# One step of Strassen's algorithm, in its seven-product form, for x times W1 in a gated cross-attention kernel

## Chip, cores, metric

The kernel runs on one core of one Trainium2 chip. The metric is the device time of one execution in microseconds. The kernel before takes 1226.47 us (median of three runs, 1226.44 to 1226.92). All data are fp32.

## The reference, cut to what matters

With x of (8, 1024, 1024), a memory of (8, 64, 512), W_mem (1024, 512) and W_gate (1024, 2048):

```python
memory_proj = einsum('bme,de->bmd', memory, W_mem)
scores = einsum('bnd,bmd->bnm', x, memory_proj) / sqrt(D)
attn = softmax(scores, axis=-1)
memory_context = einsum('bnm,bmd->bnd', attn, memory_proj)
gate_input = concatenate([x, memory_context], axis=-1)
gate = sigmoid(einsum('bnf,df->bnd', gate_input, W_gate) + b_gate)
fused = x + gate * memory_context
out = fused * rsqrt(mean(fused**2, axis=-1) + 1e-6) * norm_w
```

The gate's product splits into x times W1 (the half of W_gate for x) and memory_context times W2. The second is folded: mp times W2 plus the bias is computed once per batch, so that attn multiplies a table of 64 rows.

## The kernel before

**Setup.** TensorE transposes the memory (L133), projects it (L152, tile pm, result mpT), transposes the projection back (L169, into rows 0 to 63 of the table mg) and multiplies it by W2 (L181, tile pg2, from the tiles w2_0 and w2_1; VectorE adds the bias in L190 into rows 64 to 127 of mg). W1 is loaded into one tile, w1_sb.

**The loop.** The rows of x are handled in 32 pairs of 128-row tiles, pair q being 256 rows (t = 0 and 1). For each pair:

- `transpose_x`: VectorE turns x round in 32 by 32 blocks into xt, with 8 instructions (L203). Two buffers hold xt.
- `scores`: 16 matmuls into psT (L214), copied by ScalarE into sT (L222).
- `softmax`: a transpose on TensorE into sc (L228), then on VectorE the maximum mx (L230), the difference e (L232), on ScalarE the exponential (L233), on VectorE the sum den (L235), its reciprocal rden (L237) and attn (L240, two instructions).
- `transpose_attn`: two transposes on TensorE into pa (L249), copied by ScalarE into attnT (L251).
- `fuse`, once per t: for each of two halves h of 512 columns, 8 matmuls of x with W1 into a PSUM bank pg (L266). Then, for each h, two matmuls with a depth of 64 rows: attnT with the projection into pc (L278) and attnT with the folded table into pg (L279). ScalarE takes the sigmoid of pg (L284), VectorE multiplies it by pc (L285), adds x (L286), and ScalarE sums the squares (L287).
- `norm`: ScalarE's square root (L293), VectorE's reciprocal (L294) and scaling (L296), and the two stores.

**Order.** Nothing in the kernel before fixes an engine's order except the order in which the code is written and the scheduler of the tile framework, which may move an instruction up into a gap. In iteration q the code issues `transpose_x` and `scores` of pair q+1, `fuse(q, 0)`, `softmax` of q+1, `fuse(q, 1)`, `transpose_attn` of q+1 and `norm(q)`. Each engine runs its own queue in order.

One fp32 matmul stands in the trace as two matmul records, so a group of 8 matmuls is 16 records, and a pair's 32 matmuls with W1 are 64.

Of the kernel before, what the change touches and what calls it, by code (L numbers as in the profile page):

```python
# [14 lines left out]
P = 128  # L15
# [4 lines left out]
def tile_gated_cross_attention_rmsnorm(  # L20
# [25 lines left out]

    nc = tc.nc
# [7 lines left out]
    KE = E // P  # L55
    H = 512
# [9 lines left out]
    xgpool = ctx.enter_context(tc.tile_pool(name="xgpool", bufs=4))  # L66
    xtpool = ctx.enter_context(tc.tile_pool(name="xtpool", bufs=2))
    work = ctx.enter_context(tc.tile_pool(name="work", bufs=2))
# [35 lines left out]
    bias_sb = const.tile([P, D], F32, name="bias_sb")  # L104
# [9 lines left out]
    w1_sb = const.tile([P, KD, D], F32, name="w1_sb")  # L114
    for k in range(0, KD, 4):
        for i in range(4):
            nc.sync.dma_start(
                w1_sb[32 * i : 32 * (i + 1), k : k + 4, :], w1r[i][:, k : k + 4, :]
            )
    nw_sb = const.tile([P, D], F32, name="nw_sb")  # L120
# [73 lines left out]

    for q in range(2):
        xqs[q] = load_xq(q)
    xts, sTs, attns, attnTs = {}, {}, {}, {}
# [9 lines left out]

    def scores(q):
# [3 lines left out]
        for k in range(KD):  # L212
            for t in range(2):
                nc.tensor.matmul(  # L214
                    ps[t * M : (t + 1) * M, :],
                    mpT[:, k, b * M : (b + 1) * M],
                    xt[:, k, t * P : (t + 1) * P],
                    start=(k == 0),
                    stop=(k == KD - 1),
                )  # L220
# [4 lines left out]
    def softmax(q):  # L225

        sc = ps_sc.tile([P, 2, M], F32, tag="sc", name=f"sc{q}")
        nc.tensor.transpose(sc.rearrange("p t m -> p (t m)"), sTs.pop(q), ident)  # L228
# [16 lines left out]
    def transpose_attn(q):  # L245
        attn = attns.pop(q)
        pa = ps_sc.tile([P, 2, P], F32, tag="sc", name=f"pa{q}")
        for t in range(2):
            nc.tensor.transpose(pa[:, t, :], attn[:, t, :, :].rearrange("p i m -> p (i m)"), ident)  # L249
        attnT = small.tile([P, 2, P], F32, tag="attnT", name=f"attnT{q}")  # L250
        nc.scalar.copy(attnT, pa)  # L251
# [4 lines left out]
    def fuse(q, t):  # L256

        b = q // PPB
        if t == 0:
            sss[q] = small.tile([P, 2], F32, tag="ss", name=f"ss{q}")  # L260
        xg, xt, attnT, ss = xgs[q], xts[q], attnTs[q], sss[q]
        pgs = []
        for h in range(NH):
            pg = ps_gate.tile([P, H], F32, tag="gate", name=f"pg{q}_{t}_{h}")
            for k in range(KD):
                nc.tensor.matmul(  # L266
                    pg,
                    xt[:, k, t * P : (t + 1) * P],
                    w1_sb[:, k, h * H : (h + 1) * H],
                    start=(k == 0),  # L270
                    stop=False,
                )
            pgs.append(pg)
        pcs = []
        for h in range(NH):
            cols = slice(h * H, (h + 1) * H)
            pc = ps_ctx.tile([P, H], F32, tag="ctx", name=f"pc{q}_{t}_{h}")
            nc.tensor.matmul(pc, attnT[0:M, t, :], mg[0:M, b, cols], start=True, stop=True)  # L278
            nc.tensor.matmul(pgs[h], attnT[M:P, t, :], mg[M:P, b, cols], start=False, stop=True)  # L279
            pcs.append(pc)  # L280
        gate = work.tile([P, D], F32, tag="gate", name=f"gate{q}_{t}")
        for h in range(NH):
            cols = slice(h * H, (h + 1) * H)
            nc.scalar.activation(gate[:, cols], pgs[h], AF.Sigmoid)  # L284
            nc.vector.tensor_tensor(gate[:, cols], gate[:, cols], pcs[h], ALU.mult)  # L285
        nc.vector.tensor_tensor(xg[:, t, :], xg[:, t, :], gate, ALU.add)  # L286
        nc.scalar.activation(gate, xg[:, t, :], AF.Square, accum_out=ss[:, t : t + 1])  # L287
# [13 lines left out]

    transpose_x(0)
    scores(0)
    softmax(0)
    transpose_attn(0)
    for q in range(2):
        xgs[q] = load_xg(q)
    for q in range(NQ):
# [4 lines left out]
        if nxt:  # L313
            transpose_x(q + 1)
            scores(q + 1)
        fuse(q, 0)
        if nxt:
            softmax(q + 1)
        fuse(q, 1)
        if nxt:  # L320
# [28 lines left out]
```

## Time and profile before

| | |
|---|---|
| median of three runs | 1226.47 us |
| profiled execution, its own time | 1225.63 us |
| its span, first to last instruction | 1223.9 us |
| mean granted TensorE clock | 0.995 of full speed |
| TensorE matmul busy | 1195.8 us, 98% |
| VectorE busy | 385.8 us, 32% |
| ScalarE busy | 361.1 us, 30% |
| GpSimd busy | 0.7 us |
| HBM traffic | 93 GB/s over the span |

Spans are measured from the first instruction to the last; the execution's own time is 1.73 us longer. In the rows, PE is TensorE's matmul, PEld its weight load, DVE VectorE, ACT ScalarE, POOL GpSimd, SP the queue that issues the DMAs. A row of instructions gives line, engine, operation, output and inputs, partitions and elements, the count, busy time and mean duration, and then the idle time before them with what ended it. Matmuls overlap: the records of one run may be longer than the distance between their starts, and the distance is what a run costs.

### The profile page before, as it was taken

To read this page: it belongs to the slowest core of one execution; us is meant where nothing else is said; L and a number is where in the kernel's file an instruction comes from. 1 tells how busy PE (TensorE), PEld (TensorE's weight loads), DVE (VectorE), ACT (ScalarE), POOL (GpSimd) and SP (SyncE) were. 2 spreads that over 40 slices of the span, in tenths; PEclk is the share of its full clock that TensorE was granted. 3 is DMA by queue.
4 is the path that set the end of the run, shared out by engine and by line. 5 is a ranking of instruction groups with operands and counts; after the bars stand their busy time and mean duration, and the time that the engine had idled before them with its cause. 6 is when DMAs were issued, how large, how long until landed. Compare 5 with 4: busy or idle time off the path is not lost.

```text
span 1223.9 us, 9771 instructions
## 1 busy us (share of the span) xinstructions
PE 1195.8 (98%) x3920; PEld 541.1 (44%) x3920; DVE 385.8 (32%) x764; ACT 361.1 (30%) x531; POOL 0.7 (0%) x7
## 2 busy tenths in 40 slices
PE   7999999999999999999999999999999999999996
PEld 3444444444444444444444444444444444444442
DVE  2113333233323323233333332333233332333322
ACT  0300332333223332333223322333233323332232
POOL 0000000000000000000000000000000000000000
PEclk9999999999999999999999999999999999999998
DMA  9925132233332222333332222333322223330000
GB/s 247 217 86 138 45 84 90 91 104 103 103 103 75 76 83 78 103 103 103 103 103 69 61 94 86 104 103 103 103 83 77 74 83 98 103 103 35 35 35 34
DMA packets 57469, 113.88 MB, mean 93 GB/s; under 512 B 3920, under 2 KB 36688, under 8 KB 57424
## 3 DMA queue, kind: packets, MB, share of 16 engines
q1 hardware_dynamic: 57424, 113.26, 31.3%
q8 instruction: 31, 0.51, 0.2%
q14 instruction: 14, 0.11, 0.0%
HBM read 79.69 MB, written 33.55 MB: 93 GB/s over the span
## 4 chain that ended last, share of the span: by engine, by line
PE 91%; DVE 7%; ACT 1%; DMA 1%; issue 0%; DVEq 0%; SPq 0%; ACTq 0%
PE pg L266 73%; DVE xt L203 7%; PE pc L278 5%; PE psT L214 5%; PE pg L181 4%; PE pm L152 2%; PE sc L228 1%; DMA wm_sb<-in_w_mem_t 1%; ACT mg L172 0%; PE pt_mp L169 0%; DVE xg L296 0%; ACT L293 0%; DVE xg L286 0%; DVEq L345 0%; ACT gate L287 0%
## 5 line engine op out<-in xcount | busy, mean ns | idle before, releaser
L266 PE MATMUL pg<-w_sb,xt 128*128 128x512 f32 x2048 | 894.8, 594 | 0.0
L266 PEld LDWEIGHTS pg<-w_sb,xt 128*128 128x128 f32 x2048 | 385.5, 191 | 463.8 <-issue 463.8
L284 ACT ACTIVATE gate<-pg 128x512 f32<-128x512 f32 x128 | 76.5, 597 | 649.9 <-PE pg L279 649.9
L203 DVE STREAM_TRANSPOSE xt<-xq 128x256 f32<-128x256 f32 x256 | 87.4, 408 | 299.8 <-PE pg L266 299.8
L278 PE MATMUL pc<-mg,attnT 64*128 64x512 f32 x256 | 126.8, 615 | 0.0
L279 PE MATMUL pg<-mg,attnT 64*128 64x512 f32 x256 | 126.8, 615 | 0.0
L230 DVE TENSOR_REDUCE mx<-sc 128x2 f32<-128x128 f32 x32 | 9.4, 293 | 324.0 <-PE sc L228 324.0
L285 DVE TENSOR_TENSOR gate<-gate,pc 128x512 f32<-128x512 f32 x128 | 81.1, 671 | 33.0 <-ACT gate L284 33.0
L214 PE MATMUL psT<-xt,mpT 128*64 128x128 f32 x1024 | 77.1, 278 | 8.2 <-DVE xt L203 8.2
L284 ACT ACT_TABLE_LOAD x63 | 80.8, 1283 | 1.1
L296 DVE SCALAR_TENSOR_TENSOR xg<-xg,rstd,nw_sb 128x1024 f32<-128x1024 f32 x64 | 79.4, 1282 | 1.1
L286 DVE TENSOR_TENSOR xg<-xg,gate 128x1024 f32<-128x1024 f32 x64 | 78.1, 1221 | 1.1
L287 ACT ACTIVATE gate<-xg 128x1024 f32<-128x1024 f32 x64 | 67.7, 1057 | 35.5 <-DVE xg L286 31.2
L278 PEld LDWEIGHTS pc<-mg,attnT 64*128 64x128 f32 x256 | 42.8, 186 | 78.7 <-issue 78.7
L214 PEld LDWEIGHTS psT<-xt,mpT 128*64 128x64 f32 x1024 | 61.5, 137 | 24.4 <-DVE xt L203 12.5
L181 PE MATMUL pg<-w,mpT 128*128 128x512 f32 x128 | 55.6, 592 | 0.0
L222 ACT COPY sT<-psT 128x128 f32<-128x128 f32 x32 | 8.5, 266 | 125.5 <-PE psT L214 125.5
L279 PEld LDWEIGHTS pg<-mg,attnT 64*128 64x128 f32 x256 | 42.8, 186 | 0.0
L293 ACT ACT_TABLE_LOAD x32 | 41.1, 1283 | 0.6
L233 ACT ACT_TABLE_LOAD x31 | 39.8, 1283 | 0.6
L181 PEld LDWEIGHTS pg<-w,mpT 128*128 128x128 f32 x128 | 24.0, 190 | 28.7 <-issue 28.7
L294 DVE RECIPROCAL rstd<-rstd 128x2 f32<-128x2 f32 x32 | 5.3, 166 | 90.4 <-ACT rstd L293 90.4
(32 smaller groups left out, 207.6 us busy)
## 6 DMA issues: line engine op xcount, KB each, us to landing
xq<-in_x SPq DMA_DIRECT2D x128, 256.0 KB, 4.4
xg<-in_x SPq DMA_DIRECT2D x32, 1024.0 KB, 4.8
out<-xg SPq DMA_DIRECT2D x64, 512.0 KB, 2.7
w<-in_w_gate_t SPq DMA_DIRECT2D x8, 512.0 KB, 19.0
w_sb<-in_w_gate_t SPq DMA_DIRECT2D x8, 512.0 KB, 20.1
wm_sb<-in_w_mem_t SPq DMA_DIRECT2D x2, 1024.0 KB, 8.5
mem_sb<-in_mem SPq DMA_DIRECT2D x1, 1024.0 KB, 5.5
bias_sb<-in_b_gate SPq DMA_DIRECT2D x1, 512.0 KB, 10.8
```

Of the source, the lines that this page charges most:

```text
L181: nc.tensor.matmul(pg, mpT[:, k, q * P : (q + 1) * P], w2_sb[h][:, k, :], start=(k == 0), stop=(k == KD - 1),)
L203: nc.vector.transpose(xt[:, :, 32 * s : 32 * (s + 1)], xq[:, s, :].rearrange("p (j r) -> p j r", r=32))
L214: nc.tensor.matmul(ps[t * M : (t + 1) * M, :], mpT[:, k, b * M : (b + 1) * M], xt[:, k, t * P : (t + 1) * P], start=(k == 0), stop=(k == K ...
L266: nc.tensor.matmul(pg, xt[:, k, t * P : (t + 1) * P], w1_sb[:, k, h * H : (h + 1) * H], start=(k == 0), stop=False,)
L278: nc.tensor.matmul(pc, attnT[0:M, t, :], mg[0:M, b, cols], start=True, stop=True)
L279: nc.tensor.matmul(pgs[h], attnT[M:P, t, :], mg[M:P, b, cols], start=False, stop=True)
L284: nc.scalar.activation(gate[:, cols], pgs[h], AF.Sigmoid)
L285: nc.vector.tensor_tensor(gate[:, cols], gate[:, cols], pcs[h], ALU.mult)
L286: nc.vector.tensor_tensor(xg[:, t, :], xg[:, t, :], gate, ALU.add)
L287: nc.scalar.activation(gate, xg[:, t, :], AF.Square, accum_out=ss[:, t : t + 1])
L293: nc.scalar.activation(rstd, ss, AF.Sqrt, bias=eps_sb, scale=1.0 / D)
L296: nc.vector.scalar_tensor_tensor(xg[:, t, :], xg[:, t, :], rstd[:, t : t + 1], nw_sb, ALU.mult, ALU.mult)
```

## The change

A pair's product is a 2 by 2 block product: A11 and A12 are the first tile's rows with the first and the second half of the 1024 features (4 slices of 128 each), A21 and A22 the second tile's; B11 to B22 are the quarters of W1 (4 slices by 512 columns). Before, it takes 8 block products of 4 matmuls each. Now it takes 7, by Winograd's form of Strassen's step:

- of W1, once, in the setup: t1 = B12 - B11, t2 = B22 - t1, t3 = B22 - B12 (over B12's buffer), all three on GpSimd, and t4 = B21 - t2 on VectorE. t1 and t2 share the buffer that w2_0 had, and t4 has that of w2_1;
- of x, per pair, on VectorE (`sums`): s1 = A21 + A22, s2 = s1 - A11, s3 = A11 - A21, s4 = A12 - s2;
- the products go into three PSUM banks k1, k2, k3. k1 holds A11 B11 and then, in addition, A12 B21; k2 holds s2 t2, then also s3 t3, then also A22 t4; k3 holds s1 t1, then also s4 B22;
- the part sums that several results need are taken out of PSUM while a bank stays open: ScalarE copies k1 after its first product into p1; VectorE computes u2 = p1 + k2, u3 = p1 + k2 (after k2's second product), u3 += k3, p1 += k2 and u2 += k3;
- since a bank goes into more than one result, attnT gets a third slot, the difference of the two tiles' attn, so that the folded table's product, added to a bank that two results share, comes out right.

All matmuls and transposes of the loop are kept in program order on TensorE. `transpose_x`, `scores` and `softmax` of the next pair are called from within `fuse`, after the second, the fourth and the sixth product. Buffers change: xgpool 4 to 3, work 2 to 3 with the bias in one of its buffers during the setup, a new spool with one buffer for each of s1 to s4, p1, u2 and u3. W1 comes in 16 loads of 256 KB where it came in 8 of 512 KB. The result's residual add is now issued for t = 1 first and t = 0 after it.

The core of the diff:

```diff
-    for k in range(0, KD, 4):
+    for k, h in ((0, 0), (0, 1), (1, 1), (1, 0)):
+        t = const.tile([P, KH, H], F32, name=f"b{k + 1}{h + 1}")
...
+    nc.gpsimd.tensor_tensor(t1, b12, b11, ALU.subtract)
+    nc.gpsimd.tensor_tensor(t2, b22, t1, ALU.subtract)
+    nc.gpsimd.tensor_tensor(b12, b22, b12, ALU.subtract)
+    t3 = b12
+    t4 = big.tile([P, KH, H], F32, tag="big", name="t4")
+    nc.vector.tensor_tensor(t4, b21, t2, ALU.subtract)
...
+    def sums(q):
+        a11, a12, a21, a22 = blocks(q)
...
+        nc.vector.tensor_tensor(s1, a21, a22, ALU.add)
+        nc.vector.tensor_tensor(s2, s1, a11, ALU.subtract)
+        nc.vector.tensor_tensor(s3, a11, a21, ALU.subtract)
+        nc.vector.tensor_tensor(s4, a12, s2, ALU.subtract)
...
-        attnT = small.tile([P, 2, P], F32, tag="attnT", name=f"attnT{q}")
-        nc.scalar.copy(attnT, pa)
+        attnT = small.tile([P, 3, P], F32, tag="attnT", name=f"attnT{q}")
+        nc.scalar.copy(attnT[:, 0:2, :], pa)
+        nc.vector.tensor_tensor(
+            attnT[M:P, 2, :], attnT[M:P, 0, :], attnT[M:P, 1, :], ALU.subtract
+        )
...
+        def product(bank, lhsT, rhs, start):
+            for k in range(KH):
+                mm(bank, lhsT[:, k, :], rhs[:, k, :], start and k == 0, k == KH - 1)
...
+        product(k1, a11, b11, True)
...
+        nc.scalar.copy(p1, k1)
...
+        product(k2, s2, t2, True)
...
+        nc.vector.tensor_tensor(u2, p1, k2, ALU.add)
+        between[0]()
+        product(k1, a12, b21, False)
+        product(k2, s3, t3, False)
...
+        nc.vector.tensor_tensor(u3, p1, k2, ALU.add)
+        between[1]()
...
+        product(k3, s1, t1, True)
+        pc11 = attend(k1, 0, 0, 0)
+        pc22 = attend(k3, 1, 1, 1)
+        nc.vector.tensor_tensor(u3, u3, k3, ALU.add)
+        gated(k1, pc11, 0, 0)
+        gated(u3, pc22, 1, 1)
+        product(k2, a22, t4, False)
+        between[2]()
+        product(k3, s4, b22, False)
+        pc21 = attend(k2, 1, 0, 1)
+        pc12 = attend(k3, 0, 1, 2)
+        nc.vector.tensor_tensor(p1, p1, k2, ALU.add)
+        gated(p1, pc21, 1, 0)
+        nc.vector.tensor_tensor(u2, u2, k3, ALU.add)
+        gated(u2, pc12, 0, 1)
+        for t in (1, 0):
+            residual(t)
```

Three places show what moves. The first is TensorE over a pair, pair 1 before, from the next pair's scores on (a name's first number is the pair, those of pg and pc then give t and h):

```order
L214 MATMUL psT2_547<-xt2_538,mpT_152 64x128 x16
L266 MATMUL pg1_0_0_567<-w1_sb_103,xt1_414 128x512 x8
L266 MATMUL pg1_0_1_576<-w1_sb_103,xt1_414 128x512 x8
L278 MATMUL pc1_0_0_585<-mg_201,attnT1_522 128x512
L279 MATMUL pg1_0_0_567<-mg_201,attnT1_522 128x512
L278 MATMUL pc1_0_1_588<-mg_201,attnT1_522 128x512
L279 MATMUL pg1_0_1_576<-mg_201,attnT1_522 128x512
L228 MATMUL sc2_598<-ident_114,sT2_564 128x128
L266 MATMUL pg1_1_0_612<-w1_sb_103,xt1_414 128x512 x8
L266 MATMUL pg1_1_1_621<-w1_sb_103,xt1_414 128x512 x8
```

And pair 2 of the changed kernel, from its first product on (t12 holds t1 and t2, b12 holds t3; the second product's s2 is s2_2). All calls of `mm` carry the helper's line, L229:

```order
L229 MATMUL k1_2_720<-b11_106,xt2_597 128x512 x4
L229 MATMUL k2_2_727<-t12_360,s2_2_696 128x512 x4
L229 MATMUL k1_2_720<-b21_121,xt2_597 128x512 x4
L229 MATMUL k2_2_727<-b12_111,s3_2_697 128x512 x4
L229 MATMUL psT3_753<-xt3_734,mpT_166 64x128 x16
L229 MATMUL k3_2_772<-t12_360,s1_2_695 128x512 x4
L229 MATMUL pc2_0_0_777<-mg_215,attnT2_692 128x512
L229 MATMUL k1_2_720<-mg_215,attnT2_692 128x512
L229 MATMUL pc2_1_1_780<-mg_215,attnT2_692 128x512
L229 MATMUL k3_2_772<-mg_215,attnT2_692 128x512
L229 MATMUL k2_2_727<-t4_364,xt2_597 128x512 x4
L282 MATMUL sc3_792<-ident_128,sT3_770 128x128
```

After these come s4 B22 into k3 (4 matmuls), four more attention matmuls and the next pair's pa. The 32 matmuls with W1 have become 28, in groups of 4, and psT has moved from behind pa into the middle of the pair.

The second place is VectorE at the end of a pair, before, from a pair's first maximum to its last transposes:

```order
L230 TENSOR_REDUCE mx2_600<-sc2_598 128x2
L285 TENSOR_TENSOR gate1_0_591<-gate1_0_591,pc1_0_0_585 128x512
L285 TENSOR_TENSOR gate1_0_591<-gate1_0_591,pc1_0_1_588 128x512
L232 TENSOR_TENSOR e2_602<-sc2_598,mx2_600 128x128
L286 TENSOR_TENSOR xg1_405<-xg1_405,gate1_0_591 128x1024
L235 TENSOR_REDUCE den2_605<-e2_602 128x2
L237 RECIPROCAL rden2_607<-den2_605 128x2
L240 TENSOR_TENSOR attn2_609<-e2_602,rden2_607 128x2x64 x2
L203 STREAM_TRANSPOSE xt3_662<-xq3_531 128x8x32 x8
```

And in the changed kernel, in pair 2:

```order
L236 STREAM_TRANSPOSE xt4_871<-xq4_710 128x8x32
L285 TENSOR_REDUCE mx3_794<-sc3_792 128x2
L236 STREAM_TRANSPOSE xt4_871<-xq4_710 128x8x32
L287 TENSOR_TENSOR e3_796<-sc3_792,mx3_794 128x128
L236 STREAM_TRANSPOSE xt4_871<-xq4_710 128x8x32 x6
L290 TENSOR_REDUCE den3_799<-e3_796 128x2
L292 RECIPROCAL rden3_801<-den3_799 128x2
L258 TENSOR_TENSOR s4_3_835<-xt3_734,s2_3_833 128x512
L295 TENSOR_TENSOR attn3_803<-e3_796,rden3_801 128x2x64 x2
L377 TENSOR_TENSOR p1_2_725<-p1_2_725,k2_2_727 128x512
L379 TENSOR_TENSOR u2_2_732<-u2_2_732,k3_2_772 128x512
```

The transposes of xt for the pair after the next (xt4 while pair 2 runs) now stand among the softmax of pair 3, and s4 of pair 3 stands ahead of its attn. The sums s3, s1 and s2 of pair 3 stand earlier in the pair.

The third place is the step from the setup into the loop: on TensorE before,

```order
L181 MATMUL pg2_1_3_335<-w2_1_98,mpT_152 128x512 x8
L214 MATMUL psT0_365<-xt0_356,mpT_152 64x128
L266 MATMUL pg0_0_0_443<-w1_sb_103,xt0_356 128x512
L214 MATMUL psT0_365<-xt0_356,mpT_152 64x128 x15
L266 MATMUL pg0_0_0_443<-w1_sb_103,xt0_356 128x512
L228 MATMUL sc0_384<-ident_114,sT0_382 128x128
L266 MATMUL pg0_0_0_443<-w1_sb_103,xt0_356 128x512 x3
L249 MATMUL pa0_398<-ident_114,attn0_395 128x128 x2
L266 MATMUL pg0_0_0_443<-w1_sb_103,xt0_356 128x512 x3
```

and in the changed kernel:

```order
L198 MATMUL pg2_1_3_349<-w2_1_101,mpT_166 128x512 x8
L229 MATMUL psT0_385<-xt0_376,mpT_166 64x128 x16
L282 MATMUL sc0_404<-ident_128,sT0_402 128x128
L305 MATMUL pa0_418<-ident_128,attn0_415 128x128 x2
L229 MATMUL k1_0_446<-b11_106,xt0_376 128x512 x4
```

The first pair's matmuls with W1, which filled the gaps of its softmax, now stand behind its last transpose. On VectorE the same step is now

```order
L207 TENSOR_TENSOR mg_215<-pg2_1_3_349,bias_sb_94 64x512 x2
L220 TENSOR_TENSOR t4_364<-b21_121,t12_360 128x2048
L236 STREAM_TRANSPOSE xt0_376<-xq0_366 128x8x32 x8
L255 TENSOR_TENSOR s1_0_424<-xt0_376 128x512
L257 TENSOR_TENSOR s3_0_426<-xt0_376 128x512
L256 TENSOR_TENSOR s2_0_425<-s1_0_424,xt0_376 128x512
L258 TENSOR_TENSOR s4_0_427<-xt0_376,s2_0_425 128x512
L285 TENSOR_REDUCE mx0_406<-sc0_404 128x2
```

where before mg's last two rows were followed at once by the transposes of xt0 and these by mx0: t4 and the four sums have come between.

124 lines of the change are left out of this document (78 added, 46 removed).

## Prediction

> **What bounds the kernel now.** I read the page's busy times and the chain that ended last first:
>
> ```profile
> PE 1195.8 (98%) x3920; PEld 541.1 (44%) x3920; DVE 385.8 (32%) x764; ACT 361.1 (30%) x531; POOL 0.7 (0%) x7
> PE 91%; DVE 7%; ACT 1%; DMA 1%; issue 0%; DVEq 0%; SPq 0%; ACTq 0%
> ```
>
> TensorE has no gaps worth speaking of, and the end hangs on it nearly everywhere. So the question is what one pair costs there. Busy times of overlapping matmuls overstate that, so I cut one pair in the middle of the run at the points where TensorE changes from one kind of work to the next, and read the lengths of the stretches (the second column):
>
> ```profile
> 559.64:573.57 13.93, 13.93 (x34) 6.00 (x33) 3.13 (x4) 4.28 (x6) 0.00 (x0) 1.00 0.70 211
> 573.57:575.49 1.92, 1.92 (x10) 0.69 (x10) 0.00 (x0) 0.60 (x1) 0.00 (x0) 1.00 0.03 9
> 575.49:575.65 0.16, 0.16 (x3) 0.16 (x2) 0.00 (x0) 0.05 (x1) 0.00 (x0) 1.00 0.00 0
> 575.65:589.48 13.83, 13.83 (x33) 5.90 (x33) 3.67 (x9) 4.58 (x6) 0.00 (x0) 1.00 0.00 0
> 589.48:591.40 1.92, 1.92 (x10) 0.69 (x9) 1.81 (x6) 0.60 (x1) 0.00 (x0) 1.00 0.00 0
> 591.40:591.77 0.37, 0.37 (x5) 0.20 (x3) 0.37 (x2) 0.26 (x1) 0.00 (x0) 1.00 0.00 0
> 591.77:594.26 2.49, 2.32 (x33) 1.90 (x32) 2.46 (x5) 0.61 (x2) 0.00 (x0) 1.00 0.26 81
> sum 34.62, PE 34.45 PEld 15.54 DVE 11.44 ACT 10.96 POOL 0.00; mean PE 4.92 PEld 2.22 DVE 1.63 ACT 1.57 POOL 0.00
> ```
>
> The same for one pair near the end of the run:
>
> ```profile
> 1113.73:1148.36 34.63, 34.45 (x117) 15.55 (x116) 11.45 (x24) 10.96 (x16) 0.00 (x0) 1.00 0.08 31
> ```
>
> The first seven stretches are, in order: 32 records of x times W1, four attention matmuls, the transpose sc, 32 records again, four attention matmuls, pa, and psT. A pair costs 34.62 us, and 34.63 at the end, so it holds over the loop. VectorE works 11.44 us of it and ScalarE 10.96: both have room. What one record of x times W1 costs is read from the starts of the weight loads, the first and the last of 30 in the first stretch:
>
> ```profile
> 560.17 0.19 PEld L266 LDWEIGHTS pg<-w_sb,xt 128*128 128x128 f32 x1 [0.24 <-issue]
> ...
> 572.62 0.19 PEld L266 LDWEIGHTS pg<-w_sb,xt 128*128 128x128 f32 x1 [0.24 <-issue]
> ```
>
> 12.45 / 29 = 0.429 us. 32 of them are 13.73 us of the 13.93, and the other 0.2 is the change to the matmuls of 64 rows behind them.
>
> **The change, part by part. Four matmuls fewer per pair.** 28 in place of 32, so 8 records fewer: 8 x 0.429 = 3.43 us a pair. The groups of 4 have the same shapes, 128 by 128 by 512, and a change of bank inside the 13.83 us stretch (after 16 records) shows no gap, so I charge nothing for the six changes of bank.
>
> **psT in another place.** Today psT follows pa and waits there for the transposes of x, which are only freed to start when the last matmul with W1 is through:
>
> ```profile
> PEld psT L214 <- DVE xt L203: 12.5, 30, 0.4
> ```
>
> That is 0.40 us a pair. In the changed order the transposes for a pair are done half a pair ahead of its psT, so the wait goes. In return there is one more change of shape on TensorE, from products to psT, which I take at the 0.2 above (bounds 0 and 0.2). A pair then costs 34.62 - 3.43 - 0.40 + 0.2 = 31.0 us if nothing makes TensorE wait.
>
> **Does anything make it wait?** VectorE gets nine instructions of 512 elements and one small one per pair. The groups they resemble:
>
> ```profile
> L285 DVE TENSOR_TENSOR gate<-gate,pc 128x512 f32<-128x512 f32 x128 | 81.1, 671 | 33.0 <-ACT gate L284 33.0
> L286 DVE TENSOR_TENSOR xg<-xg,gate 128x1024 f32<-128x1024 f32 x64 | 78.1, 1221 | 1.1
> L284 ACT ACTIVATE gate<-pg 128x512 f32<-128x512 f32 x128 | 76.5, 597 | 649.9 <-PE pg L279 649.9
> L296 DVE SCALAR_TENSOR_TENSOR xg<-xg,rstd,nw_sb 128x1024 f32<-128x1024 f32 x64 | 79.4, 1282 | 1.1
> L287 ACT ACTIVATE gate<-xg 128x1024 f32<-128x1024 f32 x64 | 67.7, 1057 | 35.5 <-DVE xg L286 31.2
> L160 ACT COPY mpT<-pm 128x512 f32<-128x512 f32 x4 | 2.3, 586 | 32.8 <-PE pm L152 32.8
> ```
>
> 9 x 0.67 + 0.2 = 6.2, so VectorE comes to 17.6 of 31 us, and ScalarE with p1's copy to 11.5. Totals don't decide; the waits between do. I count from T, when pa of a pair starts. TensorE then runs pa to T+0.4, the first two products to T+7.2, needs p1 out of k1 there, and needs u2 out of k2 at T+10.7. VectorE has behind T: u2 += k3 of the pair before (0.7), two gate multiplications (1.3), two residual adds (2.4), attnT's difference (0.2): done at T+4.8. ScalarE's copy of p1 is queued behind the squares of the first residual, which is ready at about T+3.4: 3.4 + 1.1 + 0.6, so T+5.2 against 7.2. u2 then waits for the second product at T+7.2 and is there at T+8, against 10.7. The scaling (two instructions of 1.28 us) ends at T+11; u3 waits for the fourth product at T+14.1 anyway. s1 of the next pair waits for this pair's k3 product to be through, at T+19.8, with s2 behind it, and u3 += k3, queued behind them, starts when k3's attention is in, at T+22, ends at T+22.7, and is needed at T+25.5. All of this has 2 us or more to spare.
>
> The close place is the end of the pair. The last reader of xt is A22 t4; call its end E. From there VectorE has the transposes for the pair after the next, with the softmax among them, then s4, then attn, which pa needs. The rows of today:
>
> ```profile
> 575.85 0.29 DVE L230 TENSOR_REDUCE mx<-sc 128x2 f32<-128x128 f32 x1 [10.22 <-PE sc L228]
> 577.25 0.28 DVE L232 TENSOR_TENSOR e<-sc,mx 128x128 f32<-128x128 f32 x1
> 578.59 0.28 DVE L235 TENSOR_REDUCE den<-e 128x2 f32<-128x128 f32 x1
> 578.90 0.17 DVE L237 RECIPROCAL rden<-den 128x2 f32<-128x2 f32 x1
> 579.10 0.49 DVE L240 TENSOR_TENSOR attn<-e,rden 128x128 f32<-128x128 f32 x2
> 589.59 2.73 DVE L203 STREAM_TRANSPOSE xt<-xq 128x256 f32<-128x256 f32 x8 [9.99 <-PE pg L266]
> ```
>
> 0.11 until VectorE sees E (589.59 against 589.48), 2.73, then 0.29 + 0.28 + 0.28 + 0.17, s4 at 0.67, attn at 0.49, and some 0.2 of steps between: attn is there at E+5.2. TensorE reaches pa after sc (0.26 with its change), the last product (3.43 + 0.2) and four attention matmuls (1.92): E+5.8. So 0.6 us are left, and pa does not wait; p1 += k2, which is queued behind attn, is 0.3 us late, and that falls into the 2 us above. I take 0 and keep up to 0.5 us a pair for the range.
>
> **Loads.** SP's queue issues a pair's stores, then xg, then the next xq but one; each lands a good half pair ahead of its use, since transfers (the column ahead of the last in the stretches above) fill 0.70 of the first 13.93 us and little of the rest. The smaller xgpool makes xg wait for the stores of the pair three back, whose data are needed 30 us later: nothing.
>
> **The setup.** W1's sums need w2_0 free. The chain of waits and three windows (clock granted in the third column from the end) give it:
>
> ```profile
> 47.23 52.38 PE pg L181 x122
> 73.00:100.00 27.00, 26.59 (x62) 11.41 (x61) 5.07 (x8) 0.00 (x0) 0.00 (x0) 1.00 0.00 1
> 100.00:104.00 4.00, 1.40 (x3) 0.79 (x4) 3.73 (x10) 0.00 (x0) 0.00 (x0) 0.80 0.00 0
> 104.00:108.00 4.00, 4.00 (x34) 2.40 (x33) 0.00 (x0) 0.27 (x1) 0.00 (x0) 0.77 0.79 175
> ```
>
> L181 ends at 99.6; its second half, 64 records, takes 27.4 us, so w2_0 is free at 72.2, and no load is under way from 73 on. GpSimd's three subtractions of 2048 elements have no row here. The nearest is this, 0.29 us for 128 elements:
>
> ```profile
> masks.py:199 POOL TENSOR_SCALAR_AFFINE_SELECT ident<-ident 128x128 f32<-128x128 f32 x1 | 0.3, 294 | 0.0
> ```
>
> That makes 16 x 0.29 = 4.7 each as the upper bound; VectorE's 1.22 for 1024 makes 2.4 the lower one. I take 4.7, the engine's own row: 72.2 + 14.1 = 86.3, well ahead of t4 on VectorE at 101, so they cost nothing up to 14 us each for t1 and t2. The Trainium skill, GPSIMD Engine Reference, section Elementwise — side-by-side cycle accounting, gives 4497 ns for such an addition of 2048 fp32 elements, twice VectorE's time; by that the third would end at 85.7, and no run here shows it yet.
>
> What costs is VectorE's queue and TensorE's order, where the setup meets the loop:
>
> ```profile
> 101.03 2.73 DVE L203 STREAM_TRANSPOSE xt<-xq 128x256 f32<-128x256 f32 x8
> 103.19 2.08 PE L266 MATMUL pg<-w_sb,xt 128*128 128x512 f32 x2
> 105.19 2.24 PE L214 MATMUL psT<-xt,mpT 128*64 128x128 f32 x30
> 107.47 0.27 ACT L222 COPY sT<-psT 128x128 f32<-128x128 f32 x1 [57.47 <-PE psT L214]
> 108.33 0.27 PE L228 MATMUL sc<-ident,sT 128*128 128x128 f32 x1
> 110.15 0.49 DVE L240 TENSOR_TENSOR attn<-e,rden 128x128 f32<-128x128 f32 x2
> ```
>
> t4 (2 x 1.22) stands ahead of the transposes: they run from 103.5 to 106.2. psT to 108.5, sT to 108.9; from sc to the end of attn today 110.64 - 108.33 = 2.3, so attn at 111.3 and pa at 111.4. The four sums (2.7) end at 108.9, just covered by psT and sT. Until then TensorE does nothing with W1. It has also idled, and the clock falls: 0.80 and 0.77 in the windows above, 8 us with some 1.7 us lost. I charge 1.7 for the first products. The Trainium skill, TensorE: Matmul & The Clock Gate, section What's actually happening, halves the clock after an idle window of some 3.4 us and gives it back after as long a busy one; by that the loss is 1.7, or 3.4 if the wait for attn cools it again, and the sum below would be as it is or 1.7 more. The two records of 2.08 us at 103.19 agree with half speed.
>
> **The end.** The last TensorE record now starts at 1211.40:
>
> ```profile
> 1211.40 0.59 PE L279 MATMUL pg<-mg,attnT 64*128 64x512 f32 x1
> 1218.95 1.53 SPq L299 DMA_DIRECT2D out<-xg  x2
> ```
>
> From 1211.9 to 1223.9 it is 12.0 us. Now u2 += k3 comes ahead of the last sigmoid (0.7) and the residual of t = 1 ahead of that of t = 0 (1.24): 14.0.
>
> **The sum.** 111.4 + 1.7 + 32 x 31.0 - 2.5 (the last pair has no psT, sc and their change) + 14.0 = 1116.6 us of span. Done the same way, before gives a start of 106.8 for its 34.62 us pairs, so the setup costs 6.3 more, the end 2.0 more, and the pairs 115.8 less. The profiled execution lies 1.73 above its span (1225.63 and 1223.9) and the median 0.84 above that: **1119 us**.
>
> **The rivals.** *The softmax is late* (15%): VectorE's chain from E outlasts TensorE's 5.8 us, because instructions in that chain run longer beside the new PSUM reads or wait longer for each other. Each 10% on the chain is 0.5 us; beyond the 0.6 to spare it costs 31 times the excess. At +30% that is 31 x 1.0 = 31, so 1150; the case spans 1130 to 1175. For it: the chain has ten links, and only runs of eight were seen undisturbed. Against: the same instructions vary little now.
>
> *Short products break the stream* (6%): each group of 4 starts with a gap like the 0.2 us where TensorE changes shape. Six more a pair: 32 x 1.26 = 40, so 1159. Against it, no gap at the bank changes within 32 records.
>
> *Slower* (2%): the same chain from E at more than 1.8 times its length. From 5.2 to over 9.4 us TensorE waits more than 3.6 us a pair, which eats all that the pairs gain. At twice the length: 31 x 4.6 = 143, so 1262. Every instruction of it would have to slow as much, and none has been seen to.
>
> *A setup that holds the loop back* (4%): GpSimd at over 14 us an instruction keeps t4, and the transposes behind it, waiting. At 20 us each, 11 us: 1130. That the change doesn't do what it says is excluded: the order of the instructions holds the 28 matmuls.
>
> **The numbers.** The forecast as worked out has 72%, with its own range of 1110 (no cold clock, no new change of shape) to 1130 (0.4 us a pair of waiting); 1% is left for a still faster pair. For 8 in 10 the range takes in the nearer half of the late softmax: 1109 to 1146. A difference of about 0.2% is what a measurement of this kernel can tell. All cases but the slow one and a small remainder are far below that line: faster 97%, the same 1%, slower 2%.
>
> **What would show it.** Right: 56 records of products in a pair, pairs of 31.0 us, no idle time on TensorE ahead of pa, GpSimd's last subtraction over before 101 us, pa of the first pair at about 111. Wrong: pairs over 32 us; pa waiting for attn would be the late softmax, gaps ahead of each product's first weight load the broken stream, and products waiting for VectorE or for p1 a wait that I have dismissed.

## The result, and the profile after

The changed kernel takes 1106.9 us (median of four runs, 1106.69 to 1108.91) against 1226.45 us (1226.25 to 1226.92) for the kernel before: a ratio of 0.9028, with a 95% interval of 0.9013 to 0.9044. It is faster, as forecast, and by more: 119.6 us where 107 were forecast, 2 us under the low end of the range. Its profiled execution took 1106.89 us, with a span of 1105.1; the forecast for the span was 1116.6.

The page's span, busy times and chain that ended last, of the changed kernel:

```profile
span 1105.1 us, 9666 instructions
PE 1074.8 (97%) x3664; PEld 484.3 (44%) x3664; DVE 586.2 (53%) x1085; ACT 376.3 (34%) x563; POOL 14.2 (1%) x10
PE 96%; DVE 1%; ACT 1%; DMA 1%; issue 0%; DVEq 0%; SPq 0%; ACTq 0%
```

TensorE still sets the end, now for 96% of the chain, and VectorE's share of it has gone from 7% to 1% although VectorE works half as long again. One pair in the middle of the changed kernel, from the start of its pa to the start of the next pa, cut at the first record of each new kind of work on TensorE (the second column is the length, then busy time and count of PE, PEld, DVE, ACT and POOL):

```profile
572.18:572.46 0.28, 0.28 (x5) 0.28 (x4) 0.16 (x1) 0.28 (x1) 0.00 (x0) 1.00 1.16 209
572.46:586.29 13.83, 13.83 (x35) 5.90 (x33) 7.62 (x10) 5.47 (x10) 0.00 (x0) 1.00 0.48 129
586.29:588.18 1.89, 1.89 (x33) 1.72 (x32) 1.29 (x2) 0.00 (x0) 0.00 (x0) 1.00 0.74 173
588.18:591.81 3.63, 3.63 (x10) 1.44 (x8) 0.00 (x0) 1.55 (x2) 0.00 (x0) 1.00 0.49 199
591.81:593.73 1.92, 1.92 (x9) 0.69 (x8) 1.38 (x2) 0.60 (x1) 0.00 (x0) 1.00 0.00 0
593.73:597.26 3.53, 3.53 (x10) 1.58 (x9) 1.97 (x3) 1.91 (x2) 0.00 (x0) 1.00 0.00 0
597.26:597.37 0.11, 0.11 (x2) 0.10 (x1) 0.00 (x0) 0.00 (x0) 0.00 (x0) 1.00 0.00 0
597.37:600.90 3.53, 3.53 (x10) 1.34 (x8) 3.40 (x12) 1.59 (x2) 0.00 (x0) 1.00 0.00 0
600.90:602.82 1.92, 1.92 (x9) 0.69 (x8) 1.81 (x5) 0.02 (x1) 0.00 (x0) 1.00 0.48 148
sum 30.64, PE 30.64 PEld 13.73 DVE 17.63 ACT 11.42 POOL 0.00; mean PE 3.40 PEld 1.53 DVE 1.96 ACT 1.27 POOL 0.00
```

In order: pa, four products (32 records), psT, the fifth product, attention, the sixth product, sc, the seventh, attention. TensorE is busy for all of the 30.64 us; before, 0.17 of 34.62 were idle, all in the stretch of psT. Set beside the stretches of before, the 3.98 us that a pair has lost are these:

| per pair | before | after | change |
|---|---|---|---|
| 8 records of products fewer, at 0.429 | 64 | 56 | -3.43 |
| what the product stretches hold beyond 0.429 a record | 0.30 | 0.50 | +0.20 |
| psT | 2.49 | 1.89 | -0.60 |
| pa | 0.37 | 0.28 | -0.09 |
| sc | 0.16 | 0.11 | -0.05 |

The first line is what was forecast. The third was forecast at 0.40. The second was forecast at 0.20, too, but for psT's new place alone, and the last two lines, which the forecast did not look at, give most of it back.

### The profile page after: what moved, and what is told of

Its sections match the earlier page's. It is cut to its first block, busy times and chain, and to the rows that moved or that the text cites. A ratio compares the mean times of both kernels' runs of the same rounds, so it can differ in the third digit from the quotient of the medians.

```text
span 1105.1 us, 9666 instructions
## 1 busy us (share of the span) xinstructions
PE 1074.8 (97%) x3664; PEld 484.3 (44%) x3664; DVE 586.2 (53%) x1085; ACT 376.3 (34%) x563; POOL 14.2 (1%) x10
## 4 chain that ended last, share of the span: by engine, by line
PE 96%; DVE 1%; ACT 1%; DMA 1%; issue 0%; DVEq 0%; SPq 0%; ACTq 0%
PE k L229 71%; PE pc L229 11%; PE psT L229 6%; PE pg L198 5%; PE pm L169 2%; PE pa L305 1%; DMA wm_sb<-in_w_mem_t 1%; ACT mg L189 0%; PE sc L282 0%; DVE xt L236 0%; DVE xg L346 0%; DVE t L220 0%; PE pt_mp L186 0%; DVE xg L391 0%; ACT L388 0%
## 5 line engine op out<-in xcount | busy, mean ns | idle before, releaser
L229 PE MATMUL k<-t,s 128*128 128x512 f32 x512 | 233.4, 598 | 0.0
L229 PE MATMUL k<-b,xt 128*128 128x512 f32 x512 | 231.9, 596 | 0.0
L229 PE MATMUL k<-b,s 128*128 128x512 f32 x512 | 230.2, 592 | 0.0
L229 PEld LDWEIGHTS k<-b,s 128*128 128x128 f32 x512 | 94.9, 190 | 116.6 <-issue 116.6
L229 PEld LDWEIGHTS k<-t,s 128*128 128x128 f32 x512 | 94.7, 190 | 112.9 <-issue 112.9
L229 PEld LDWEIGHTS k<-b,xt 128*128 128x128 f32 x512 | 95.4, 191 | 108.2 <-issue 108.2
L229 PE MATMUL k<-mg,attnT 64*128 64x512 f32 x256 | 126.8, 615 | 0.0
L229 PE MATMUL pc<-mg,attnT 64*128 64x512 f32 x256 | 126.8, 615 | 0.0
L229 PE MATMUL k<-t,xt 128*128 128x512 f32 x256 | 118.4, 605 | 0.0
L255 DVE TENSOR_TENSOR s<-xt 128x512 f32<-128x512 f32 x32 | 22.2, 692 | 131.5 <-PE k L229 131.4
L229 PEld LDWEIGHTS pc<-mg,attnT 64*128 64x128 f32 x256 | 42.8, 186 | 78.7 <-issue 55.9
L229 PEld LDWEIGHTS k<-t,xt 128*128 128x128 f32 x256 | 46.0, 189 | 70.2 <-issue 46.7
L229 PE MATMUL psT<-xt,mpT 128*64 128x128 f32 x1024 | 65.3, 280 | 5.8 <-DVE xt L236 5.8
L229 PEld LDWEIGHTS psT<-xt,mpT 128*64 128x64 f32 x1024 | 57.1, 139 | 30.5 <-issue 29.5
```

The costliest lines, as they stand in the source:

```text
L229: nc.tensor.matmul(o, lhsT, rhs, start=start, stop=stop, skip_group_check=True)
L255: nc.vector.tensor_tensor(s1, a21, a22, ALU.add)
```

## The experiments

Two theories stood after the result. *The wait*: psT's place was worth 0.6 us a pair, because it waited there for the transposes of x, and the rest is eight records. *The rival*: more of the gain comes from elsewhere, from the shorter stream or from VectorE's new order, and psT's place was worth the 0.40 that its row showed.

### psT moved in the kernel before

Only this is changed: psT of the next pair comes between the two column halves of the first tile's product, so that x is turned round by then.

```diff
-            scores(q + 1)
-        fuse(q, 0)
+        fuse(q, 0, (lambda q=q + 1: scores(q)) if nxt else None)
...
+            if h == 0 and mid is not None:
+                mid()
```

> The kernel before, with 8 products, but with the next pair's psT between the two halves of the first tile instead of right behind pa. Theory (the changed kernel's extra gain lies in psT: clear of the transposes of x its stretch costs 1.9 us where it costs 2.49 before, and pa 0.1 less): pairs of 34.62 - 0.60 - 0.09 + 0.1 for one more change of shape = 34.0 us, time about 1226 - 18 = 1208. Rival (the forecast's term was right, 0.40 for the wait less 0.2 for the change of shape, and the rest of the gain comes from the products): pairs of 34.4, time about 1220.

Measured: 1208.35 us (1206.28 to 1209.17) against 1224.44 on the same chip, ratio 0.9861 (0.9844 to 0.9878). Two psT, a pair apart, in the chain of that kernel (start, length):

```profile
555.40 1.90 PE psT L214 x32
...
589.43 1.90 PE psT L214 x32
```

A pair is 589.43 - 555.40 = 34.03 us, 0.59 less than the 34.62 of before, and in the same chain the two halves around psT are 6.87 and 7.06, together the 13.93 that they were. So the whole difference is psT's 2.49 that became 1.90, and psT between products costs nothing for a change of shape. The rival's 34.4 falls. In the time, 31 x 0.59 would be 18.3 us. The profiled execution, 1206.28 us, lies 18.2 below 1224.44 and the median 16.1, since the four runs spread over 2.9 us; what varies is taken up below.

### psT right behind pa, in the changed kernel

If only the wait counted, the old place must cost nothing once x is ready there.

```diff
-            fuse(q, (first, second, third))
+            first()
+            second()
+            fuse(q, (nothing, nothing, third))
```

> The changed kernel with psT put back right behind pa, its transposes of x still done before. Theory (what psT lost is the wait for the transposes, not its neighbours): pairs of 30.6 to 30.8, time 1106 to 1111. Rival (the place between products is what made psT cheaper): the psT stretch is back at about 2.4, pairs of 31.1 to 31.2, time about 1122.

One execution: 1112.57 us. The pair, and then the chain at the start:

```profile
547.73:578.37 30.64, 30.64 (x110) 13.84 (x111) 17.63 (x34) 11.62 (x18) 0.00 (x0) 1.00 0.36 103
```

```profile
107.91 6.07 DMA xq<-in_x
114.21 2.74 DVE xt L236 x8
117.00 3.67 PE psT L229 x30
120.67 17.36 PE k L229 x40
```

The pair is the same 30.64: once x is ready the place costs nothing, and the wait was all. The change of shape from products to psT, which the forecast charged with 0.2, costs nothing on balance either, since it is gone here. The total is 5.7 us longer, and that is at the start: psT of pair 1 now stands ahead of pair 0's products and waits for its transposes and their load, so that in the chain the products begin at 120.67 instead of 111.26. The setup itself also ended 2.2 us later in this execution, which is taken up below.

### Eight products again

One product is issued twice, with the same output (work repeated, everything else as in the changed kernel).

```diff
         product(k3, s1, t1, True)
+        product(k3, s1, t1, True)
```

> The changed kernel with the product s1 t1 issued twice over (the second starts the bank afresh), so 32 matmuls with W1 per pair as before, with all sums. Theory (TensorE alone bounds the pair and nothing of the sums is on its path): 8 records of 0.429 more, pairs of 34.08, time 1107 + 110 = 1217; the 0.54 left to the pair of before is psT's place. Rival (part of the pair is bound by VectorE's sums, which the added matmuls would cover): less than 110 us more, under 1200 if a us per pair is.

One execution: 1218.7 us, and the pair

```profile
571.64:605.72 34.08, 34.08 (x118) 15.26 (x119) 17.63 (x33) 11.43 (x17) 0.00 (x0) 1.00 0.33 93
```

34.08 - 30.64 = 3.44 us for eight records. VectorE's 17.63 us are all still there, and the eight records are added in full: a product's price is TensorE's alone, and the sums cost nothing as long as VectorE keeps up.

### How far is pa from waiting?

The forecast's close place was attn ahead of pa, with 0.6 us to spare. The instructions that write attn are repeated, to lengthen exactly that chain, four times and two times.

```diff
-        for i in range(2):
+        for i in list(range(2)) * 4:
```

> The changed kernel with attn written four times over, so VectorE's chain ahead of pa is 3 x 0.49 = 1.47 us longer. Theory (0.6 us to spare between attn and pa): pa comes 0.9 late, 31 x 0.9 = 27 us more, 1134. Rival 1 (the chain isn't near TensorE's path): no change, 1107. Rival 2 (nothing to spare, pa was on the edge): 31 x 1.47 = 46 more, 1152.

> The changed kernel with attn written twice, 0.49 us more ahead of pa. Theory (0.6 us to spare): hidden, 1107 to 1108. Rival (less than 0.2 to spare): 31 x 0.3 = 9 us or more, 1116 and up.

Four times: 1128.87 us, a pair of 31.25. Its chain, at the end of a pair, and its waits (us in total, times, longest):

```profile
583.22 1.62 DVE attn L295 x8
584.84 0.14 issue
584.98 0.41 PE pa L305 x2
```

```profile
PE pa L305 <- DVE attn L295: 20.5, 31, 3.3
```

The chain now runs over VectorE. Eight instructions took 1.62 us, two take 0.49 in the changed kernel: 1.13 longer for a pair that is 0.61 longer, so 0.52 us were to spare. The expected total was too long because a repeated attn was charged at the full price of the pair of them; the slack, which was the question, is what was forecast. Two times: 1107.37 us and

```profile
556.19:586.83 30.64, 30.64 (x109) 13.73 (x111) 17.89 (x35) 11.39 (x17) 0.00 (x0) 1.00 0.36 103
```

Hidden, as it had to be. The rival that the softmax is late was some 0.5 us of VectorE's time away, and no more.

### The start: t4 on GpSimd, and TensorE's order left free

What the setup still costs is VectorE's t4 ahead of the first transposes, and the first pair's products kept behind its softmax. Each is undone alone, and both together.

```diff
-    nc.vector.tensor_tensor(t4, b21, t2, ALU.subtract)
+    nc.gpsimd.tensor_tensor(t4, b21, t2, ALU.subtract)
```

```diff
-        tc.keep_in_program_order(
-            nc.tensor.matmul(o, lhsT, rhs, start=start, stop=stop, skip_group_check=True)
-        )
+        nc.tensor.matmul(o, lhsT, rhs, start=start, stop=stop, skip_group_check=True)
```

(the same for sc and pa). Left free, the scheduler changes TensorE's order in the first pair alone.

> The changed kernel with t4 on GpSimd instead of VectorE. Theory (t4's 2.3 us stand on the path from the setup to the first psT, and GpSimd has until the first A22 t4 at 134 us for its 4.5): 2.3 us less, 1104.6. Rival (the wait is set by something else there): 1106.9.

> The changed kernel without the fixed program order on TensorE, so that the scheduler may move products into gaps; it does so in the first pair alone, where the first product and part of the second stand among psT, sc and pa. Theory (program order costs only the first pair's idle time behind psT, 108 to 111 us, with a clock that stays up): 2 to 4 us less, 1103 to 1105; pairs of 30.65 as they are. Rival (the products moved up only run at the low clock and push psT back): 0, 1107.

> Both together, t4 on GpSimd and the free order on TensorE. Theory: the two gains add, 4 to 6 us, 1101 to 1103. Rival (they fill the same idle time): no more than the better one alone, 1104.

| | time, us | setup ends | psT of pair 1 | between |
|---|---|---|---|---|
| changed kernel | 1106.9 | 97.96 | 126.70 | 28.74 |
| t4 on GpSimd | 1106.7 (one execution) | 100.36 | 126.54 | 26.18 |
| order left free | 1104.0 (one execution) | 99.70 | 123.81 | 24.11 |
| both | 1102.07 (1101.52 to 1102.21) | 100.69 | 122.05 | 21.36 |

"Setup ends" is the start of VectorE's last two rows of mg, which no edit comes ahead of. The two rows of both together from which its line comes, from the timeline and from the chain:

```profile
100.69 1.39 DVE L207 TENSOR_TENSOR mg<-pg,bias_sb 64x512 f32<-64x512 f32 x2 [5.47 <-PE pg L198]
```

```profile
122.05 1.90 PE psT L228 x32
```

By the last column the order is worth 4.6 us, t4 2.6, both 7.4. By the total, t4 alone brought nothing, because its setup happened to end 2.4 us later. With both edits the kernel takes 0.8997 (0.8982 to 0.9012) of the time before on the same chip, 1224.39: the fastest version here.

Whether t4 is worth 2.6 us was tried again, the changed kernel and t4 on GpSimd on one chip.

> The changed kernel as it is, to stand beside the next one on the same chip. Theory (the end of the setup moves from run to run by up to 2.7 us with the clock that TensorE has in its first 64 records of pm): times between 1106.5 and 1109.2, in both kernels' runs alike. Rival (each program has its own fixed setup): times within 0.3 us of each other.

> The changed kernel with t4 on GpSimd once more, timed. Theory (t4's 2.3 to 2.5 us lie on the path, and the first look hid them behind a setup that ended 2.4 us later): median 2.0 to 2.6 us under the changed kernel's of the same chip, 1104.5. Rival (no gain): the same median within 0.5 us.

The changed kernel took 1108.55 (1107.15 to 1109.05), with t4 on GpSimd 1107.41 (1104.28 to 1107.79); ratios 0.9044 (0.9032 to 0.9056) and 0.9028 (0.9013 to 0.9043). The medians are 1.1 apart, where 2.0 to 2.6 were expected, and the runs overlap. The changed kernel alone moved by 1.9 us, so the rival of a fixed setup for each program falls. From the setup's end to psT of pair 1 it was now 28.49 and 27.73, only 0.8 apart. Cut at psT of pair 0 (the start of its last 30 records), the traces agree with each other:

| | setup's end to psT of pair 0 | from there to psT of pair 1 | granted clock there |
|---|---|---|---|
| changed kernel | 6.39 | 22.35 | 0.83 |
| t4 on GpSimd | 4.19 | 21.99 | 0.86 |
| changed kernel, again | 6.38 | 22.11 | 0.85 |
| t4 on GpSimd, again | 4.20 | 23.53 | 0.74 |

Up to psT, t4 is worth 2.2 us, both times. Behind it TensorE ran below full speed for a while, at the lowest clock in the last execution, which took 1.4 us longer there than the changed kernel beside it. What t4 is worth in the total stays unsettled.

### What varies at the start

The suspect is TensorE's clock. In the version with both edits, the weight loads of the first projection (start, length, idle time ahead of it) read

```profile
14.48 0.34 PEld L169 LDWEIGHTS pm<-memT,wmp 128*128 128x128 f32 x1 [0.52 <-issue]
15.33 0.34 PEld L169 LDWEIGHTS pm<-memT,wmp 128*128 128x128 f32 x1 [0.52 <-issue]
15.99 0.19 PEld L169 LDWEIGHTS pm<-memT,wmp 128*128 128x128 f32 x1 [0.32 <-issue]
16.42 0.19 PEld L169 LDWEIGHTS pm<-memT,wmp 128*128 128x128 f32 x1 [0.24 <-issue]
```

Up to 15.9 us a record takes 0.85 us, from there on 0.43: half speed, then full. The granted clock in the windows reads 1.00 all the while, so the distance between the records' starts (their pitch) is what shows it. In the changed kernel's profiled execution the pitch is 0.43 already at 11.9 us. The whole stretch, from the two chains, first the changed kernel's and then that of both edits:

```profile
10.81 27.50 PE pm L169 x64
```

```profile
11.27 29.77 PE pm L169 x64
```

From pm's end to the setup's end it is 59.65 us in both. So what differs lies in the first 40 us: 2.27 us in pm, and 0.46 in the last transposes of the memory ahead of it.

To test it, TensorE was kept busy by matmuls of the identity with itself, which nobody reads: ahead of the first transposes and again in the gap ahead of the first psT, on top of both edits.

```diff
+    def idle(name, n):
+        pw = ps_ctx.tile([P, P], F32, tag="ctx", name=name)
+        for _ in range(n):
+            nc.tensor.matmul(pw, ident, ident, start=True, stop=True)
...
+    idle("warm0", 40)
...
+    idle("warm1", 24)
```

> The kernel with t4 on GpSimd and the free order, with 40 matmuls of the identity with itself on TensorE before the first transposes and 24 more behind the last of the folded table's products; they write a PSUM tile that nothing reads. Theory (the clock is low there because TensorE idles): pm's 64 records always take 27.5 us, psT of the first pair 1.9 to 2.2 and no product runs slow; 2 to 4 us under the 1102, so 1098 to 1100, with a small spread. Rival (the clock at the start follows something else, or the added matmuls hold back what they precede): 1101 to 1103.

Measured: 1103.79 us (1103.47 to 1103.96), a ratio of 0.9007 (0.8994 to 0.9019). The clock does what the theory says: pm took 27.47, and psT of pair 0 1.89 instead of 3.06. The small spread proves nothing: these four runs lie within 0.5 us of each other, but those with both edits alone lay within 0.7. And it isn't faster than without the added matmuls (1102.07). Two things took the gain back. The scheduler had moved VectorE's copies of W_mem ahead of memT, and the second two of them wait for their load:

```profile
11.55 1.29 DVE L165 COPY wmp<-wm_sb 128x1024 f32<-128x1024 f32 x2 [1.42 <-DMA wm_sb<-in_w_mem_t]
```

So in the chain pm starts at 14.16 us where it started at 11.27 with both edits, 2.89 later for the 2.30 that it is shorter. The first group of added matmuls would have held pm back, too: behind it the transposes of the memory began at 11.97, where they began at 6.40 with both edits. And the second group stood in the way of psT:

```profile
101.07 5.52 PE L149 MATMUL warm<-ident 128*128 128x128 f32 x48
```

It ended at 106.6, while xt had been ready at 105.4. From the setup's end to psT of pair 1 it is 22.04 us, against 21.36 with both edits. Fewer were tried, 24 and 10.

> As a_warm, with 24 added matmuls at the start and 10 behind the setup in place of 40 and 24. In a_warm each took 0.27 us, so the 40 ended at 12.1 us, 2 us after the first transposes could have begun, and the 24 held psT back from 103.7 to 106.5. Theory (the clock needs TensorE busy, and fewer matmuls that end before their successors' data arrive cost nothing): the 24 end at 8 us, the 10 at 103.4; the full clock stays, the setup ends at 98 to 98.5, psT of the first pair at 101.5 to 104; 3 to 4 us under a_best, 1098 to 1099. Rival (fewer matmuls no longer hold the clock): 1101 to 1102 as a_best.

1102.78 us (1102.59 to 1103.91), ratio 0.9 (0.8984 to 0.9016): still not under 1102.07, and above what was expected. The theory holds for the second group: psT of pair 0 takes 1.89, and from the setup's end to psT of pair 1 it is now 19.73 us, 1.6 better than 21.36. For the first group the rival came in. The 24 were over at 9.6 us and the first transposes of the memory began at 9.40, but VectorE's copies stand in the same order as in the run before, and TensorE waits for memT ahead of the last transposes:

```profile
13.40 0.94 PE L156 MATMUL pt_mem<-ident,mem_sb 128*128 128x128 f32 x4 [2.52 <-DVE memT L159]
```

```profile
14.34 28.88 PE pm L175 x64
```

After 2.52 us without work TensorE was at half speed again (a granted clock of 0.58 from 13 to 17 us), and pm took 28.88, not 27.5. The setup ended at 102.86, 2.2 us later than with both edits. A version with the added matmuls and VectorE's old order was not tried.

## Why the prediction was right, and where it was not

**Right: the eight records.** 8 x 0.429 = 3.43 us a pair, no gap at the changes of bank; the pair with eight products gives 3.44.

**Right: nothing makes TensorE wait.** VectorE works 17.63 us a pair (17.6 forecast), ScalarE 11.42 (11.5). From T = 572.18, p1's copy ended at T+5.0 (5.2) and u2 at T+8.1 (8). The end of the pair, on VectorE and TensorE, in the changed kernel's timeline:

```profile
566.83 0.45 DVE L236 STREAM_TRANSPOSE xt<-xq 128x256 f32<-128x256 f32 x1 [1.55 <-PE k L229]
...
570.37 0.69 DVE L258 TENSOR_TENSOR s<-xt,s 128x512 f32<-128x512 f32 x1
570.98 0.49 DVE L295 TENSOR_TENSOR attn<-e,rden 128x128 f32<-128x128 f32 x2
...
572.18 0.44 PE L305 MATMUL pa<-ident,attn 128*128 128x128 f32 x2
```

The transposes start at 566.83, so by the forecast's 0.11 E is 566.72. attn is there at E+4.75 (forecast 5.2) and pa starts at E+5.46 (5.8). Both came some 0.4 us earlier than counted, and the difference is 0.7; less the 0.14 from attn's end to pa that the lengthened chain shows, 0.57 to spare, where 0.6 was forecast and the lengthened chain gave 0.52.

**Right: GpSimd's subtractions are hidden.** The last of the three, at 4.51 us where 4.7 was taken (the Trainium skill's GPSIMD Engine Reference, section Elementwise — side-by-side cycle accounting, states 4497 ns for 2048 fp32 elements, and the trace agrees):

```profile
79.61 4.51 POOL L217 TENSOR_TENSOR b<-b,b 128x2048 f32<-128x2048 f32 x1
```

It is over at 84.1, t4 begins at 99.4.

**Wrong in size: the step "That is 0.40 us a pair".** The wait of psT was there, and it went, but its price was read from a row that gives only how long the weight loads stood idle. The start of psT in the kernel before, weight loads and matmuls:

```profile
591.76 0.19 PEld L214 LDWEIGHTS psT<-xt,mpT 128*64 128x64 f32 x2 [0.17 <-issue]
591.77 0.43 PE L214 MATMUL psT<-xt,mpT 128*64 128x128 f32 x2
...
592.37 1.72 PEld L214 LDWEIGHTS psT<-xt,mpT 128*64 128x64 f32 x30 [0.41 <-DVE xt L203]
592.37 1.96 PE L214 MATMUL psT<-xt,mpT 128*64 128x128 f32 x30 [0.17 <-DVE xt L203]
...
594.26 1.98 PE L266 MATMUL pg<-w_sb,xt 128*128 128x512 f32 x4
```

The first matmul, two records, starts at 591.77, because it needs only the first tile's half of xt. The next one needs the second tile's and waits until 592.37. From there the 30 records take 1.89 us, which is what all 32 take in the changed kernel, where nothing waits (586.29 to 588.18). So the early start of two records gains nothing, and the wait costs the whole distance from 591.77 to 592.37, 0.60 us. psT's stretch lost 0.60, and moving psT alone took 0.59 off the pair of the kernel before. The row's 0.41 begins only where the first two weight loads are over. The matmuls have an idle time of their own, 0.17, and it ends at the same 592.37: it is the end of the same wait, and adding it to the other would count it twice. The page had one more sign. VectorE's 7% of the chain that ended last are, in its list by line, the transposes of L203, some 86 us or 2.7 a pair: it was VectorE that released psT, pair after pair.

In the changed kernel psT's matmuls wait for xt twice, at the start, where before they did 31 times; and pa waits for attn once, 2.1 us in the first pair. The loop has neither:

```profile
PE psT L229 <- DVE xt L236: 5.8, 2, 5.2
```

**Wrong in size and in place: the new change of shape.** It was taken at 0.2, from products to psT. The table's +0.20 is that number by luck. The product stretch behind psT holds 0.20 more than its records in both kernels (13.93 before, 3.63 after). New are 0.10 in the products that now stand between pa and psT, and 0.10 in the sixth product, which now stands between attention and sc. The neighbours give most of it back: pa costs 0.28 ahead of a product and 0.37 ahead of psT, sc 0.11 behind a product and 0.16 behind attention. That leaves 0.06, so the term was 0.14 too high. For pa the runs show it (0.37 again with psT put back behind it in the changed kernel, 0.27 with a product behind it in the kernel before); that sc's 0.05 comes from its neighbour was only argued.

Together the 0.20 of the wait and the 0.14 of the shapes make, but for rounding, 30.64 of 31.0: 32 x 0.36 = 11.5 us, the whole 11.5 us by which the span was missed. The other terms err by little and cancel, in us of span:

| | forecast | measured |
|---|---|---|
| pa of the first pair | 111.4 | 110.82 |
| loss of the first products at the lower clock | 1.7 | 1.8 |
| 32 pairs | 992.0 | 980.5 |
| psT and sc missing in the last pair | -2.5 | -2.1 |
| the end | 14.0 | 14.2 |
| span | 1116.6 | 1105.1 |

The rows behind the measured column, from the changed kernel's timeline: pa of the first pair, the first product and the second, and the last record of TensorE.

```profile
110.82 0.44 PE L305 MATMUL pa<-ident,attn 128*128 128x128 f32 x2 [2.10 <-DVE attn L295]
111.10 5.31 PE L229 MATMUL k<-b,xt 128*128 128x512 f32 x8
116.24 3.60 PE L229 MATMUL k<-t,s 128*128 128x512 f32 x8
...
1090.39 0.59 PE L229 MATMUL k<-mg,attnT 64*128 64x512 f32 x1
```

The same 8 records take 5.31 us and then 3.60, which is the 1.7; and pa at 572.18 is 15 pairs of 30.64 and 1.76 behind pa at 110.82, so all the other loss lies there too. From 1090.9, counted as in the prediction, to 1105.1 it is 14.2.

That pa came near its forecast is partly luck. The setup ended 1.7 us earlier than in the profile of before (97.96 against 99.62), and psT of the first pair took longer than the 2.24 that was taken from before, where matmuls of the first product stood ahead of most of it and kept TensorE going. The chain's row and four windows of the changed kernel:

```profile
104.35 3.69 PE psT L229 x30
```

```profile
98.00:104.00 6.00, 0.66 (x2) 0.29 (x2) 5.97 (x11) 0.00 (x0) 0.00 (x0) 0.80 0.00 0
104.00:108.00 4.00, 3.65 (x30) 3.27 (x30) 2.88 (x5) 0.00 (x0) 0.00 (x0) 0.50 0.61 135
108.00:112.00 4.00, 1.54 (x6) 0.82 (x6) 1.82 (x7) 0.95 (x3) 0.00 (x0) 0.93 1.06 243
112.00:116.24 4.24, 4.24 (x7) 1.73 (x6) 2.73 (x8) 0.00 (x0) 0.00 (x0) 0.61 0.41 152
```

After six microseconds in which TensorE was busy for 0.66, it ran at half speed, with a granted clock of 0.50. The clock came back (0.93 from 108 to 112 us), while TensorE was busy for 1.54 of four microseconds, and fell again in the first product, to 0.61. So time was lost twice, some 1.8 us in psT and 1.7 in the first product. The sum charged one loss of 1.7; the other case that the prediction gives, 3.4 if the wait for attn cools TensorE again, is the one that came. And 0.84 us were added because the median of before lay that much above its profiled execution; after, the two agree within 0.01.

**The range** ended at 1109 because its lower end took the wait as known and left only the change of shape and the cold clock open. The shape's bounds of 0 and 0.2 held what was measured. The wait had none, and with 0.60 in its place the same sum gives some 1113, inside the range. None of the rivals came in. (The broken stream's 1159 was worked out with 0.21 us a gap; with the 0.2 that it names it is 1157, and nothing hung on it.)

**Where the gain came from.** Of 3.98 us a pair, 3.4 are the algorithm's (eight records, less 0.06 for the changes of shape), and 0.6 psT's place, which the kernel before could have had by itself: 16.1 of its 1224.4 us.

## What to carry to other kernels

An engine that has no gaps is measured by the distance between equal points one iteration apart. A wait on it is measured the same way: by the length of the stretch that holds it, against the same stretch where nothing waits. The idle time in a row of waits can be less than what the wait costs, because work that started early and then stopped gains nothing. When a change of algorithm also moves a step, move the step alone in the old kernel, too, since its share may be had without the rest. Slack found by arithmetic is cheap to check: repeat the last instruction of the chain until the loop gets longer.

## What the runs showed of the hardware

The time of the start varies from execution to execution by more than some edits are worth. With the same setup code, the first projection's 64 records took between 27.50 and 29.77 us, and the setup ended between 97.96 and 100.69, because the half speed at the beginning was over by 10.2 us in one execution (four records of the memory's transpose that began there took 0.66 us, against 1.12 with both edits) and lasted until 15.9 in another. The Trainium skill, TensorE: Matmul & The Clock Gate, section What's actually happening, states that TensorE is at half clock until it has been busy for a window, and that the window runs freely, so that the same kernel starts at another phase each time. The trace agrees: half pitch, varying in length, and none of it in pm when added matmuls kept TensorE busy until the transposes ahead of it; with 2.52 us of idle TensorE in between, half speed was back. With both edits the granted clock of the windows read 1.00 there and did not show it; it did show 0.50 at 104 to 108 us in the changed kernel.

A stretch of products between other shapes takes 0.1 to 0.2 us more than its records: 3.63 us for 8 of them between psT and attention, 3.53 between attention and sc, against 8 x 0.429 = 3.43. A neighbour can take less in return: psT in the middle of the products and psT right behind pa gave the same pair of 30.64 us.

psT's matmuls for the two tiles gain nothing from one of them starting early: 30 of its 32 records, after a wait, take the same 1.89 us as all 32.

VectorE's small instructions of one kind cost less in a row than a pair of them suggests: 1.62 us for eight attn, 0.49 for two, so 0.19 for each further one.
